# Second encoder layer of the phase attention: one shared PSUM tile for keys and queries, and a Tanh that writes both halves of the partitions

## The chip, the cores and the metric

The kernel runs on one core of a Trainium2 chip. The metric is the device time of one execution in microseconds (us). Before the change it is 3364.57 us, the median of 5 runs (3363.05 to 3370.61).

A core has five engines with instruction queues of their own, each worked off in order: TensorE (PE, matrix products; its weight loads are shown apart as PEld), VectorE (DVE), ScalarE (ACT, which evaluates functions such as Tanh and Gelu), GpSimd (POOL) and SyncE (SP, which here issues most transfers). Products land in PSUM, a memory of 128 partitions that ACT and DVE can read; everything else works in SBUF, also of 128 partitions.

## What is computed

The program is a tokenizer, one transformer layer with window attention and a mixture of experts, and a second layer that consists of a "phase" attention and an LSTM over 569 time steps, for 16 sequences of width 256. The change lies in the phase attention. Cut to what matters:

```python
def encode(W1, b1, W2, b2):                       # W1 256x256, W2 256x64
    h = gelu(x @ W1 + b1)
    return tanh(h @ W2 + b2)
key_phase   = encode(Wk1, bk1, Wk2, bk2) * freq * pi      # freq: 1, 2, 4, 8 by 16 columns
query_phase = encode(Wq1, bq1, Wq2, bq2) * freq * pi
key_phasor  = cos(key_phase)   + 1j * sin(key_phase)
query_conj  = cos(query_phase) - 1j * sin(query_phase)
memory    = cumsum(key_phasor[..., None] * V[:, :, None, :], axis=1)
retrieved = real(sum(memory * query_conj[..., None], axis=2))
...                                               # scaled, normalized, times Wo, added to x
```

Its result, added to the rows and normalized again, is the input of the LSTM:

```python
gates = x_t @ W_ih.T + h @ W_hh.T + b             # for each of 569 steps
i, f, g, o = split(gates, 4)
c = sigmoid(f) * c + sigmoid(i) * tanh(g)
h = sigmoid(o) * tanh(c)
```

## The kernel before

The rows are kept in tiles of 128 rows by 256 columns. For the second layer, the 569 positions are cut into blocks: block 0 of 32 steps, blocks 1 to 8 of 64 steps, block 9 of 25. Chunk 8 of the row tiles holds the short blocks 0 and 9, chunks 0 to 7 hold blocks 1 to 8. A batch is one chunk of 8 of the 16 sequences, so every block is fed by two batches, and a batch is worked by two slots of two row tiles each.

Four kinds of work run together in the last half of the program (from about 1590 us on):

- **front()** (from line 1339), 36 calls: loads two row tiles, adds the experts' outputs, normalizes, turns the tile (`ftr`, `fxT`), and runs the encoders: first layer `ek`/`eq` with Gelu into `gk`/`gq`, then `v`, then the second layer into the PSUM tile `z` (lines 1405 to 1413), Tanh into `y` (named `fy`, line 1416), and three DVE operations that scale, round and subtract (lines 1420 to 1425) and leave the phase in turns in PHI. fronts() then applies Sin to a whole batch of PHI on ACT (line 1635), after a one-element Silu (line 1632).
- **back()** (from line 1472): takes PHI and V of a batch, computes the retrieval as masked products within the tile (`sc`, `w`, `r`) and with the running state S (`ds`), normalizes, multiplies with Wo (`po`), normalizes again and multiplies with W_ih (`xm`); the result `xp` goes to memory as the LSTM's input (`XCD`, `XOD`).
- **steps()**: the LSTM. A step is a chain over PE, ACT and DVE: products of the hidden state with W_hh into the PSUM tiles `gates` and `out_gate` (lines 1741 and 1750) on top of the input that ACT has copied there (lines 1690 and 1695), Tanh of the gates (line 1762) and of the output gate (1770), three DVE operations (1777 to 1790), Tanh of the cell (1798), and the new hidden state `X` (1805). After the Tanh the gates are cleared for the next step by a product with zeros (1684). The input of a block is loaded into `xc` and `xo` once both batches' backs are done with it.
- **sums_of()**: the cumulative sums behind the LSTM.

The order in which these are interleaved is not left to the hardware: class Order is a planner that runs while the program is built. Every piece yields the engine it needs and its cost in us just before its instruction is issued; the planner keeps a time at which each engine becomes free, and always takes the piece that can start first. The LSTM's step has due times of its own (table STEP), and another piece is put ahead of it only if it fits before them, give or take an allowance (`spare`) that depends on how far the backs are ahead of the LSTM. A change of the function table on ACT counts as 1.3 us in the plan. What the plan fixes is the order of instructions on each engine; on the chip each waits for its data by semaphores.

Why the keys' and queries' phases take 128 partitions: cos and sin of the same phase are both needed, and they come from one Sin over 128 partitions, the upper half with a quarter turn added (`off` is 0.25 on partitions 0 to 63 and 0 on 64 to 127). So the 64 values of the second layer have to stand twice, on partitions 0 to 63 and again on 64 to 127. Before the change the product makes both: the weights `Wk2` and `Wq2` are loaded twice side by side into tiles of [128, 2, 2, 64], and product() splits the 128 output partitions into four matmuls of 32 weight columns each (line 1085). z is [128, 2, 256]: 128 partitions, keys and queries side by side, 256 rows of data:

```python
for i, name in enumerate(("k", "q")):
    yield "ACT", 0.45
    nc.scalar.activation(y[:, i, :], z[:, i, :], AF.Tanh, bias=col(f"b{name}2"))
```

The biases' columns (`bk2`, `bq2`) hold the 64 values twice as well.

Of the kernel before, what the change touches and what calls it, by code (L numbers as in the profile page):

```python
# [10 lines left out]
F32 = mybir.dt.float32  # L11
BF16 = mybir.dt.bfloat16
AF = mybir.ActivationFunctionType
# [100 lines left out]
COLUMN = 0.00169  # L114
# [180 lines left out]
def kernel(ctx: ExitStack, tc: tile.TileContext, a: dict, out: bass.AP):  # L295
    nc = tc.nc
# [13 lines left out]
    def col(name, i=0, lo=0, hi=128):  # L310
        return cols[lo:hi, COL[name] + i : COL[name] + i + 1]
# [4 lines left out]
    def frow(name, n=D, at=0):  # L316
        return flow[:, FLOW[name] + at : FLOW[name] + at + n]
# [32 lines left out]
    slot = route.tile([128, NP, 2, NC], F32, name="slot")  # L350
# [635 lines left out]
    l1w = bg.enter_context(tc.tile_pool(name="l1w", bufs=1))  # L986
    Wih = l1w.tile([128, 2, 4 * D], F32, name="W_ih")
    l1 = {n: l1w.tile([128, 2, D], F32, name=n) for n in ("Wk1", "Wq1", "Wv", "Wo")}
    for n in ("Wk2", "Wq2"):
        l1[n] = l1w.tile([128, 2, 2, 64], F32, name=n)  # L990
    masks = l1w.tile([128, 2, 128], F32, name="masks")
    none = l1w.tile([128, 1], F32, name="none")
    S = [l1w.tile([128, 2, 2, D], F32, name=f"S{p}") for p in range(0, NP, 2)]
# [1 line left out]
    def cell_columns(w):  # L995
        return w.rearrange("p (i r) -> p i r", i=2)[:, :, :384].rearrange("p i (a x) -> p i a x", a=4)

    def out_columns(w):
        return w.rearrange("p (i r) -> p i r", i=2)[:, :, 384:]

    def prepare(mo):

        yield "at", ("tile", 0, 1)

        def kxn(n):
            return a[n].rearrange("(k p) n -> p k n", p=128)

        lb = S[0].rearrange("p i k d -> p (i k d)")
        nc.sync.dma_start(lin, kxn("W_lin"))
        for t, of in ((lstm_b, 0), (lb, 1)):  # L1010
            nc.sync.dma_start(t, a["lstm_b"][of].to_broadcast([128, 4 * D]))
        nc.sync.dma_start(Whh, kxn("W_hh"))
        nc.sync.dma_start(Wih, kxn("W_ih"))
        for n in ("Wk1", "Wq1", "Wv", "Wo"):
            nc.sync.dma_start(l1[n], kxn(n))
        for n in ("Wk2", "Wq2"):
            for i in range(2):
                nc.sync.dma_start(l1[n][:, :, i, :], kxn(n))
        nc.sync.dma_start(masks, a["masks"].rearrange("p (i n) -> p i n", i=2))
        yield "at", ("tile", 0, 12)  # L1020
        yield "DVE", 0.2
        nc.vector.tensor_tensor(shut, frow("b_lin", 1), frow("b_lin", 1, 1), ALU.subtract)
        yield "DVE", 0.2
        nc.vector.tensor_scalar(shut, shut, 2.0, None, ALU.mult)
        yield "DVE", 0.2
        nc.vector.tensor_tensor(lin[:, :, :1], lin[:, :, 1:], lin[:, :, :1], ALU.subtract)
        yield "DVE", 0.4
        nc.vector.tensor_copy(wl, lin[:, :, :1].to_broadcast([128, 2, 128]))
        by_unit = [cols[:, COL[n] : COL[n] + 2] for n in ("fw", "bw")]
        yield "DVE", 0.2  # L1030
        nc.vector.tensor_tensor(weights[:, 0, :], by_unit[0], by_unit[1], ALU.subtract)
        for i, of, by in ((0, weights[:, 0, :], 0.5), (1, by_unit[1], -0.5), (2, by_unit[1], 0.5)):
            yield "DVE", 0.2
            nc.vector.tensor_scalar(weights[:, i, :], of, by, None, ALU.mult)
        for t in begins.values():
            yield "POOL", 0.6
            nc.gpsimd.memset(t, 1.0)
            nc.gpsimd.memset(t.rearrange("p (b t) -> p b t", b=NB)[:, :, :1], 0.0)
        for t in XS_OF:
            yield "POOL", 1.0  # L1040
            nc.gpsimd.memset(t.rearrange("p k t x -> p (k t x)"), 0.0)
        yield "POOL", 0.2
        nc.gpsimd.memset(nil, 0.0)
        for t in XO:
            yield "POOL", 0.5
            nc.gpsimd.memset(t.rearrange("p t x -> p (t x)"), 0.0)
        yield "DVE", 0.2
        nc.vector.memset(one3, 1.0)
        nc.vector.memset(none, 0.0)
        yield "DVE", 1.2  # L1050
        nc.vector.tensor_tensor(lstm_b, lstm_b, lb, ALU.add)
        yield "DVE", 0.5
        v = cell_columns(lstm_b)[:, :, :, 64:]
        nc.vector.tensor_scalar(v, v, 2.0, None, ALU.mult)
        for n, t in bias3.items():
            yield "DVE", 0.3
            nc.vector.memset(t, 0.0)
            x = frow(n)[:1]
            pieces = mo.tile([1, 3, D], BF16, name=n + "_pieces", tag="pieces", bufs=1)
            left = S[1][:1, 0, 0, :]  # L1060
            yield "DVE", 1.4
            nc.vector.tensor_copy(pieces[:, 0, :], x)
            nc.vector.tensor_tensor(left, x, pieces[:, 0, :], ALU.subtract)
            nc.vector.tensor_copy(pieces[:, 1, :], left)
            nc.vector.tensor_tensor(pieces[:, 2, :], left, pieces[:, 1, :], ALU.subtract)
            for i in range(3):
                for j in range(2):
                    nc.sync.dma_start(t[i : i + 1, j, :], pieces[:, i, :])

        for k in range(2):
            for v in (cell_columns(Whh[:, k, :])[:, :, :, :64], out_columns(Whh[:, k, :])):
                yield "POOL+", 1.3
                nc.gpsimd.tensor_scalar(v, v, 0.5, None, ALU.mult)
            yield "POOL+", 0.85
            v = cell_columns(Wih[:, k, :])[:, :, :, 64:]
            nc.gpsimd.tensor_scalar(v, v, 2.0, None, ALU.mult)

    def product(out, lhsT, rhs, start, stop):  # L1080


        for m in range(0, out.shape[0], 32):
            own = slice(m, min(m + 32, out.shape[0]))
            nc.tensor.matmul(out[own], lhsT[:, own], rhs, start=start, stop=stop)  # L1085

    def bank(name, slot):
        return ps.tile([128, 512], F32, name=name, tag=f"bank{slot}", bufs=1)
# [178 lines left out]
    def copy(to, src, scale=None, bias=None):  # L1267

        if plan.chosen == "DVE":
            if scale is None:  # L1270
                nc.vector.tensor_copy(to, src)  # L1271
            else:
                nc.vector.tensor_scalar(to, src, scale, bias, ALU.mult, ALU.add)
        elif scale is None:
            nc.scalar.copy(to, src)
        else:
            nc.scalar.activation(to, src, AF.Identity, scale=scale, bias=bias)
# [61 lines left out]
    def front(p, c, n, at, slot):  # L1339

        u = f"{p}_{c}"
# [8 lines left out]
        for j in range(2):  # L1350
            y = wk.tile([128, 2, D], F32, name=f"yg{u}_{j}", tag=f"yg{slot}_{j}")
# [20 lines left out]
        g = {}  # L1372
# [23 lines left out]
        for j in range(2):  # L1396
            for k in range(2):
# [3 lines left out]
                    start=False, stop=(j + k == 2),  # L1401
                )
        yield "DVE/ACT", 0.69, 0.58
        copy(V[:, both, :], v)
        z = bank(f"z{u}", slot).rearrange("p (k n) -> p k n", k=2)
        y = wk.tile([128, 2, 256], F32, name=f"fy{u}", tag=f"xn{slot}")
        for i, name in enumerate(("k", "q")):
            for k in range(2):
                yield "PE", 256 * COLUMN
                product(  # L1410
                    z[:, i, :], l1[f"W{name}2"][:, k].rearrange("p i x -> p (i x)"),
                    g[name][:, k, :], start=(k == 0), stop=(k == 1),
                )
        for i, name in enumerate(("k", "q")):
            yield "ACT", 0.45
            nc.scalar.activation(y[:, i, :], z[:, i, :], AF.Tanh, bias=col(f"b{name}2"))


        yield "DVE+", 0.54
# [200 lines left out]
    def fronts(slot):  # L1620
        for n, (c, p0, late) in enumerate(BATCHES):
            if late:
                continue
            yield "rank", n - 2
            yield from front(p0 + 2 * slot, c, n, 2 * slot, slot)
            batch = batches[n]
            plan.mark(("front", n, slot))
            if slot:
                yield "at", ("front", n, 0)

                yield "ACT", 0.2, "silu"
                nc.scalar.activation(none, none, AF.Silu)
                for i in range(2):
                    yield "ACT", 0.6, "silu"
                    nc.scalar.activation(batch[0][:, i, :], batch[0][:, i, :], AF.Sin, scale=-2.0 * PI_BELOW)
                if c == 8:
                    nc.sync.dma_start(PHD[:, :, 128 * p0 : 128 * p0 + 512], batch[0])
                    nc.sync.dma_start(VD[:, p0 : p0 + 4, :], batch[1])
                plan.mark(("phi", n))
# [283 lines left out]
    n, total = sums[len(RUNS) - 1]  # L1923
# [152 lines left out]
```

## Time and profile before

| what | value |
|---|---|
| median of 5 runs | 3364.57 us |
| the profiled execution, its time | 3363.43 us |
| its span, first to last instruction | 3361.7 us |
| mean granted TensorE clock | 0.978 |
| PE busy | 3058.7 us, 91% of the span |
| PEld busy | 2231.1 us, 66% |
| DVE busy | 2027.6 us, 60% |
| ACT busy | 1470.0 us, 44% |
| POOL busy | 786.3 us, 23% |
| first z product starts at, last | 1601.7 us, 2937.4 us |
| LSTM: first and last Tanh of the gates start at | 1709.7 us, 3317.0 us |

A group's row in the profile names the line, the engine, the operation, what it writes and reads, the shapes and the count; behind the bar stand its busy time, the mean ns of one, and the idle time of its engine just before it with what ended that. Each matmul of this program leaves two records in the trace, so counts of matmuls there are twice those of the program. PE is pipelined: what a row of products takes is best read from where the next one starts, since the ends are modelled and overlap.

### The profile page before, as it was taken

How to read it: one execution, taken by the hardware profiler on the slowest of the kernel's cores; microseconds unless marked ns; L12 is line 12 of the kernel's file. 1: busy time of each engine (PE TensorE's matmuls, PEld its weight loads, DVE VectorE, ACT ScalarE, POOL GpSimd, SP SyncE). 2: the span in 40 equal slices, each digit the busy share in tenths (PEclk: the TensorE clock that was granted, in tenths of full speed). 3: DMA queues.
4: the chain of work that ended last, by engine and by line, in shares of the span. 5: the costliest groups of instructions: out<-in, count | busy, mean ns of one | idle time of the engine just before them, and what ended most of it. 6: DMA issues, size and time to landing. Idle time of an engine off the chain costs nothing.

```text
span 3361.7 us, 134328 instructions
## 1 busy us (share of the span) xinstructions
PE 3058.7 (91%) x57536; PEld 2231.1 (66%) x57536; DVE 2027.6 (60%) x6787; ACT 1470.0 (44%) x5030; POOL 786.3 (23%) x1524
## 2 busy tenths in 40 slices
PE   6999999999759999997899999999999999999884
PEld 3666666666548888886566666766666666666652
DVE  4677777766732222222566777777777777766555
ACT  3545545554412222221443555555555555454442
POOL 1253554444533322222311011000101010100000
PEclk9999999999979999998999999999999999999997
DMA  5111221111176666663333333333323333333333
GB/s 179 53 53 52 88 79 62 48 36 41 42 261 225 226 225 233 225 234 126 112 92 89 93 76 89 83 95 75 98 75 92 83 92 78 76 92 79 90 102 113
DMA packets 276071, 366.81 MB, mean 109 GB/s; under 512 B 144481, under 2 KB 220177, under 8 KB 263313
## 3 DMA queue, kind: packets, MB, share of 16 engines
q1 hardware_dynamic: 249360, 300.91, 30.6%
q0 software_dynamic: 14496, 39.75, 3.1%
q10 hardware_dynamic: 11616, 17.56, 1.8%
q8 instruction: 451, 7.39, 0.9%
q14 instruction: 148, 1.20, 0.1%
HBM read 239.33 MB, written 118.75 MB: 107 GB/s over the span
## 4 chain that ended last, share of the span: by engine, by line
PE 38%; DVE 7%; ACT 4%; issue 2%; DMA 1%; SPq 1%; POOL 0%; ACTq 0%; DVEq 0%
PE gates L1741 13%; PE xm_False L1085 5%; PE out_gate L1750 2%; PE ek L1085 2%; PE z L1085 2%; PE eq L1085 2%; PE po_False L1085 2%; PE ds_False L1085 1%; PE v L1085 1%; ACT act L1762 1%; PE r_False L1085 1%; ACT th L1798 1%; DVE ab L1777 1%; DVE cT L1790 1%; DVE act L1783 1%
## 5 line engine op out<-in xcount | busy, mean ns | idle before, releaser
L1741 PE MATMUL gates<-W_hh,X 128*32 128x96 f32 (+1 forms) x18176 | 488.3, 248 | 63.6 <-DVE X L1805 61.4
L1741 PEld LDWEIGHTS gates<-W_hh,X 128*32 128x32 f32 (+1 forms) x18176 | 374.1, 103 | 257.8 <-DVE X L1805 243.3
L1248 ACT ACTIVATE hT<-hp,w 128x256 f32<-128x256 f32 x316 | 132.3, 471 | 480.4 <-PE hp L1241 313.3
L1762 ACT ACTIVATE act<-gates 128x96 f32<-128x96 f32 x568 | 141.7, 249 | 446.0 <-PE gates L1741 439.0
L1255 PE MATMUL y<-w,hT 128*128 128x256 f32 x1264 | 289.7, 382 | 5.2 <-ACT hT L1248 1.5
L1085 PE MATMUL xm_False<-W_ih,dxT_False 128*32 128x256 f32 x4352 | 292.1, 380 | 2.5 <-DVE dxT_False L1271 1.9
L1241 PE MATMUL hp<-xt,w 128*128 128x256 f32 x1264 | 287.8, 381 | 1.0 <-ACT hT L1248 1.0
L1777 DVE SCALAR_TENSOR_TENSOR ab<-act 128x64 f32<-128x64 f32 x568 | 127.9, 225 | 259.7 <-ACT act L1762 250.1
L1255 PEld LDWEIGHTS y<-w,hT 128*128 128x128 f32 x1264 | 236.8, 190 | 45.2 <-ACT hT L1248 14.4
L1684 PEld LDWEIGHTS <-nil 128*32 128x32 bf16 x4552 | 189.2, 94 | 112.5 <-issue 53.7
L1241 PEld LDWEIGHTS hp<-xt,w 128*128 128x128 f32 x1264 | 240.1, 191 | 35.7 <-ACT hT L1248 1.4
L1184 POOL DMA_INDIRECT YT<-ys,to x158 | 153.3, 970 | 439.6 <-DVE ys L1261 408.1
L1261 DVE TENSOR_TENSOR ys<-y,w 128x512 f32<-128x512 f32 x79 | 54.6, 691 | 316.4 <-PE y L1255 223.9
L1750 PE MATMUL out_gate<-W_hh,X 128*32 128x64 f32 x9088 | 233.7, 220 | 1.7 <-issue 1.7
L1690 ACT COPY gates<-xc 128x96 f32<-128x96 f32 x569 | 138.7, 244 | 185.5 <-DMA xc<-XCD 77.8
L1750 PEld LDWEIGHTS out_gate<-W_hh,X 128*32 128x32 f32 x9088 | 187.4, 110 | 4.8 <-issue 2.0
L1805 DVE SCALAR_TENSOR_TENSOR X<-toT,th 128x32 f32<-128x32 f32 x569 | 109.9, 193 | 120.9 <-ACT th L1798 117.4
L1798 ACT ACTIVATE th<-cT 128x32 f32<-128x32 f32 x569 | 130.5, 229 | 92.5 <-DVE cT L1790 43.3
L1301 POOL TENSOR_SCALAR d_False_rstd<-d_False_mv 128x2 f32<-128x2 f32 (+1 forms) x36 | 9.0, 251 | 675.8 <-DVE d_False_mv L1293 551.5
L908 POOL DMA_INDIRECT XS<-XN,at x144 | 149.0, 1035 | 45.6 <-issue 24.4
L693 PE MATMUL wqk<-wxT,wqkv 128*128 128x128 f32 x1152 | 150.6, 278 | 8.8 <-ACT wxT L687 8.6
L693 PEld LDWEIGHTS wqk<-wxT,wqkv 128*128 128x128 f32 x1152 | 139.4, 192 | 24.9 <-ACT wxT L687 13.5
(356 smaller groups left out, 6498.6 us busy)
## 6 DMA issues: line engine op xcount, KB each, us to landing
w<-in_wpack SPq DMA_DIRECT2D x79, 1154.0 KB
taps<-in_taps SPq DMA_DIRECT2D x16, 1764.0 KB
xc<-XCD SPq DMA_DIRECT2D x71, 384.0 KB
XCD<-xp_False SPq DMA_DIRECT2D x256, 96.0 KB
xs<-XS SPq DMA_DIRECT2D x79, 258.0 KB
yg<-YT SPq DMA_DIRECT2D x72, 256.0 KB
HD<-h SPq DMA_DIRECT2D x72, 128.0 KB
fh<-HD SPq DMA_DIRECT2D x72, 128.0 KB
```

The costliest lines, as they stand in the source:

```text
L693: nc.tensor.matmul(qk[:, j, m, :], wqkv[:, k, D * j + 128 * m : D * j + 128 * m + 128], xT[:, k, :], start=(k == 0), stop=(k == 1),)
L908: fill(0, nc.gpsimd.indirect_dma_start(out=XS[0], out_offset=bass.IndirectOffsetOnAxis(ap=at[:, i, c - lo : c - lo + 1], axis=0), in_=XN[p ...
L1085: nc.tensor.matmul(out[own], lhsT[:, own], rhs, start=start, stop=stop)
L1184: keep(nc.gpsimd.indirect_dma_start(out=YT, out_offset=bass.IndirectOffsetOnAxis(ap=to[:, i : i + 1], axis=0), in_=ys[:, i, :], in_offset= ...
L1241: nc.tensor.matmul(hp[:, i, :], w1[:, k, hc * 128 : (hc + 1) * 128], xT[:, k, :], start=(k == 0), stop=(k == 1),)
L1255: nc.tensor.matmul(y[:, i, :], hT[:, hc, 128 * i : 128 * i + 128], w2[:, hc, :], start=(hc == 0), stop=(hc == 3),)
L1684: nc.tensor.matmul(g[32 * q : 32 * q + 32, :n], nil[:, :32], nil[:, :n], start=True, stop=last)
L1741: nc.tensor.matmul(GC[32 * q : 32 * q + NB * (1 + half), :96], before[:, kk, NB * (1 - half) :], Whh[:, kk, own : own + 96], start=False, ...
L1750: nc.tensor.matmul(GO[32 * q : 32 * q + 32, :64], before[:, kk, :], Whh[:, kk, own : own + 64], start=False, stop=(kk == 1),)
L1762: nc.scalar.activation(act[:, :96], GC[:, :96], AF.Tanh, scale=0.5), begun.pop((k, t))
L1777: nc.vector.scalar_tensor_tensor(ab, act[:, :64].rearrange("p (g x) -> p g x", g=2), 1.0, act[:, 64:].rearrange("p (g x) -> p g x", g=2), ...
L1798: nc.scalar.activation(th.rearrange("p k x -> p (k x)"), cT, AF.Tanh, scale=0.5)
```

## The change

The second layer's weights of keys and queries share one tile, `W2`, keys in columns 0 to 63 and queries in columns 64 to 127; each is loaded once. The product for keys writes partitions 0 to 63 of z and that for queries partitions 64 to 127, so z is [128, 256]. The loop over the two halves of the 256 contracted values (k) is now the outer one. Tanh then reads the 64 partitions of one encoder and is run twice for each: once to the same half of the partitions of y, once to the other half. The planner is told of two pieces of PE work instead of four, and of four on ACT instead of two. What follows (the scaling, rounding and Sin) is the same.

```diff
-    for n in ("Wk2", "Wq2"):
-        l1[n] = l1w.tile([128, 2, 2, 64], F32, name=n)
+    l1["W2"] = l1w.tile([128, 2, 2, 64], F32, name="W2")
...
-        for n in ("Wk2", "Wq2"):
-            for i in range(2):
-                nc.sync.dma_start(l1[n][:, :, i, :], kxn(n))
+        for i, n in enumerate(("Wk2", "Wq2")):
+            nc.sync.dma_start(l1["W2"][:, :, i, :], kxn(n))
...
-        z = bank(f"z{u}", slot).rearrange("p (k n) -> p k n", k=2)
+        z = bank(f"z{u}", slot)[:, :256]
         y = wk.tile([128, 2, 256], F32, name=f"fy{u}", tag=f"xn{slot}")
+        for k in range(2):
+            yield "PE", 256 * COLUMN
+            for i, name in enumerate(("k", "q")):
+                product(
+                    z[64 * i : 64 * i + 64], l1["W2"][:, k, i, :], g[name][:, k, :],
+                    start=(k == 0), stop=(k == 1),
+                )
         for i, name in enumerate(("k", "q")):
-            for k in range(2):
-                yield "PE", 256 * COLUMN
-                product(
-                    z[:, i, :], l1[f"W{name}2"][:, k].rearrange("p i x -> p (i x)"),
-                    g[name][:, k, :], start=(k == 0), stop=(k == 1),
-                )
-        for i, name in enumerate(("k", "q")):
-            yield "ACT", 0.45
-            nc.scalar.activation(y[:, i, :], z[:, i, :], AF.Tanh, bias=col(f"b{name}2"))
+            own = slice(64 * i, 64 * i + 64)
+            for half in (i, 1 - i):
+                yield "ACT", 0.45
+                nc.scalar.activation(
+                    y[64 * half : 64 * half + 64, i, :], z[own], AF.Tanh,
+                    bias=col(f"b{name}2", 0, own.start, own.stop),
+                )
```

Since the planner's input changes, the order of all instructions on PE, DVE and ACT in the last half of the program is planned anew.

## The prediction

> **What bounds the kernel now.** I read the page first, then the kernel in stretches, then the order of time around one stall. From the page's costliest groups and the groups by line, the parts the change touches and the wait that matters:
>
> ```profile
> L1690 ACT COPY gates<-xc 128x96 f32<-128x96 f32 x569 | 138.7, 244 | 185.5 <-DMA xc<-XCD 77.8 <-PE gates L1684 68.2 <-PE out_gate L1684 24.6
> L1085 PE MATMUL z<-gq,Wq 128*32 128x256 f32 x576 | 43.1, 383 | 0.0
> L1085 PE MATMUL z<-gk,Wk 128*32 128x256 f32 x576 | 41.1, 382 | 2.7 <-DVE V L1271 1.5 <-ACT V L1275 1.1
> L1416 ACT ACTIVATE fy<-z,cols 128x256 f32<-128x256 f32 x72 | 30.6, 465 | 11.8 <-PE z L1085 11.7
> ```
>
> Each row: busy us, mean ns of one, idle before it and its cause. z has 1152 records for 36 calls of front(), 32 a call (each written matmul leaves two records); its two Tanh a call take 465 ns each. The first row is the recurrent layer (LSTM) fetching its input: 77.8 us of ACT's idle time there ends with the landing of xc, which the flow (fronts and backs) has to produce. Next, three stretches: inside a block of 64 steps, a block's start, and the end, when no front or back is left.
>
> ```profile
> 2297.00:2357.00 60.00, 56.71 (x1795) 40.49 (x1796) 48.53 (x188) 33.05 (x138) 5.42 (x12) 1.00 0.31 79
> 2369.00:2385.00 16.00, 15.79 (x306) 9.61 (x298) 12.27 (x30) 3.47 (x12) 1.56 (x5) 1.00 0.44 109
> 3200.00:3300.00 100.00, 80.35 (x2616) 54.54 (x2607) 48.60 (x220) 43.32 (x202) 0.00 (x0) 1.00 0.26 74
> ```
>
> Columns: length, busy us of PE, PEld, DVE, ACT, POOL, then the granted clock (1.00 throughout). The cell's Tanh (L1762) starts 40 times in the last stretch, 2.50 us a step, with nothing else to do; inside the block 23 times in 60 us, 2.55 a step, although PE carries all the flow's products. So a step is its own dependency chain, and the flow's products ride in its gaps. But in the second stretch, 16 us, the recurrence stands and PE is 99% busy. In order of time, ACT and then PE:
>
> ```profile
> 2368.93 0.25 ACT L1762 ACTIVATE act<-gates 128x96 f32<-128x96 f32 x1 [1.27 <-PE gates L1741]
> ...
> 2382.63 0.24 ACT L1690 COPY gates<-xc 128x96 f32<-128x96 f32 x1 [11.04 <-DMA xc<-XCD]
> ...
> 2384.84 0.25 ACT L1762 ACTIVATE act<-gates 128x96 f32<-128x96 f32 x1 [0.65 <-PE gates L1741]
> ```
>
> ```profile
> 2371.86 1.91 PE L1085 MATMUL xm_False<-W_ih,dxT_False 128*32 128x256 f32 x32
> 2373.59 1.91 PE L1085 MATMUL ek<-fxT,Wk 128*32 128x256 f32 x32
> ...
> 2383.04 1.07 PE L1085 MATMUL z<-gk,Wk 128*32 128x256 f32 x16 [0.21 <-DVE V L1271]
> 2383.93 0.84 PE L1741 MATMUL gates<-W_hh,X 128*16 128x96 f32 x32
> 2384.81 0.61 PE L1085 MATMUL z<-gq,Wq 128*32 128x256 f32 x8
> ```
>
> The last xm, which the next block's input is made of, ends at 2373.77; the input lands 8.9 us later (9.5 at 2204.63, 10.2 at 1849.46), and PE works off other products meanwhile, z just ahead of the gates. From the starts of L1762, all 568 intervals: 550 last at most 3.2 us (mean 2.57, sum 1412), 18 are longer (sum 196). Seven of these stand before a block: 57.6 us before block 1, then 13.2, 19.2, 15.9, 16.0, 15.9, 15.9; none before block 8. The recurrence starts at 1709.7. So time can be won in two places: that start, and these stalls.
>
> **The change part by part.** *z on PE.* 32 records of 256 columns start 1.73 us apart from the next group (2371.86 to 2373.59). After the change a front issues half of them: 0.87 us less, times 36 = **31.2 us of PE**. No row shows this z, where two strips stream gk and two gq. The bounds: concurrent as now (0.87 a front saved), or the two halves one after the other (nothing saved). I take the first; the gates row L1741 also streams other columns of W_hh into each strip.
>
> *Tanh on ACT.* 72 of 128x256 become 144 of 64x256. Shape prices: 366 ns (L737, a 64x256 copy) to 465 ns (L1416). No row writes another half of the partitions than it reads; below I bound that by nothing and by twice 465. I take 465. Two in a row take 0.84 us, so 36 x 0.84 = **30 us more on ACT**. Cover: in a step ACT is done with the recurrence 1.43 us after L1762's start and next needed at 2.50, free for 1.07 us. 26 ordinary steps carry two Tanh today: median 2.505 us, against 2.504 for the 294 without any flow work on ACT. If that cover went, it would be 0.42 us for each Tanh past it. Behind a Tanh wait the recurrence's next copy and Tanh on ACT, and, through the gates, PE.
>
> The page TensorEngine Tiling (PSUM Bottleneck) of the Trainium skill speaks against the change: a faster TensorE does not speed up reading PSUM out, which may become the limit. By that rule a front's stage goes from 1.73 (PE) to 1.68 (ACT), 2 us in all and not 31.
>
> *Loads.* Two DMAs fewer of 4 among the weights on SP, issued in the expert stage, some 600 us ahead; nothing, since z first runs at 1601.7. If late they would hold the first z.
>
> *The order.* The planner redoes the whole order, as the built instructions show, and this decides. I priced each row of PE's order as above (128-wide turns 0.11 each) and cut it at the gates of each step. Sum from the first front: 825.7 us before, 794.6 after, 31 less as it must be. Where it goes:
>
> - Ordinary steps: 599.6 to 584.7 us. Worth nothing: steps with 0 and with 1.2 to 1.3 us of products both average under 2.58.
> - The start: up to the last xm of block 0, 82.5 to 75.8, so -6.7. But ACT's order there has 16 table loads where there were 8, since Gelu of the next front now stands between the two Sin of a batch. At 1.28 us that is 10.3 us on ACT in two clumps. Ahead of the first's readers PE has some 12 us of other products, and behind the second the input takes 15.3 us to land (last xm 1693.9, copy 1709.2), so both are mostly covered. Bounds -6.7 to +3.6; I take **-5**.
> - The stalls. Products in them (us) against length: 50.6 gives 57.6; 11.3, 13.2; 16.7, 19.2; 13.2, 15.9. So content plus 7 at the first, plus 1.9 to 2.7 elsewhere. New content: 48.3, 9.9, 16.0, 18.4, 16.9, 4.1, 5.8. By these offsets (2.5 for the last two): 55.3, 11.7, 18.5, 21.1, 19.6, 6.6, 8.3; changes -2.3, -1.4, -0.6, +5.2, +3.6, -9.3, -7.6. Before block 8 there is a new one: its last xm now stands one step ahead, not ten. With 9.3 us to land, less the rest of a step, that interval is about 10.3 instead of 2.5: +7.8. Three steps that took 3.8 with a table load and 2.6 us of products lose those products: -2. Sum **-6.6**; -14 if the new one is hidden, -1.5 if the stalls before 6 and 7 stay at 10.
>
> The page ScalarE: Activation LUTs (What ACT_TABLE_LOAD costs) puts a switch at 1283 ns plus a drain of 1380. The trace shows the first and not the second: after the load at 1644.06 the next ACTIVATE starts at 1645.35. By the page the 8 loads would be 21 us, by the row 10.
>
> *Sum:* -5 - 6.6 = -11.6, about -12. The profiled execution took 3363.43 us (span 3361.7 and 1.7 around it), 1.1 under the median: 3351.4 on its scale, **3353** on the median of 3364.57.
>
> **The rivals.**
> *All of it comes back (0.12).* The flow is what the stalls wait for, so 31.2 us less of PE end in them: 3333. For: PE is 99% busy there. Against: the order leaves 15 us of the saving in ordinary steps.
> *No change (0.23).* The table loads eat the gain at the start (0) and the stalls before blocks 6 and 7 wait for transfers at 10 us (-1.5): 3363. The same follows if the mixed strips of z don't run together. For: ACT has 10.3 us more in some 100 us. Against: the cover counted above.
> *Slower (0.10).* A Tanh that reads one half and writes the other takes twice as long, 0.93 us. The order puts two or three Tanh into each of 54 intervals; a pair would take 1.8 and miss the 1.07 free by some 0.75, 40 us in all: 3353 + 40 = 3393. For: no such write in the trace. Against: the plain ones cost no more than a copy. It decides from a pair of about 1.42 us on: 54 x 0.35 = 19 turns -12 into +7.
>
> **How the numbers follow.** Forecast, 0.55: 3353, own range 3344 to 3362. This kernel's measurement can tell about 0.2%, 6.7 us, so faster means under 3357.8, slower over 3371.3. Faster: nine tenths of the forecast, the first rival, and some of the second: 0.65. Same: 0.24. Slower: 0.11. The range reaches down most of the way to the first rival and up past no change: 3336 to 3367; it leaves out the slower rival and the last of the first.
>
> **What would show it.** z with 576 records and some 40 us busy, fy x144 at 0.37 to 0.47 us; L1762's first start at 1700 to 1707; steps still at 2.50 where two Tanh sit; stalls of 19 to 21 us before blocks 4 and 5, under 9 before 6 and 7, about 10 before 8. I am wrong if fy is over 0.6 us, if the start is later than 1710, if the stalls before 6 and 7 stay over 12, or if the mean ordinary step moves from 2.57 by over 0.02 (11 us).

## The result, and the profile after

The changed kernel takes 3375.92 us, the median of 28 runs (3368.41 to 3382.92); the kernel before, run beside it, 3367.83 us (50 runs, 3362.89 to 3373.82). The ratio is 1.0022, 95% interval 1.0016 to 1.0027: slower by some 8 us, where 12 us faster were forecast. The profiled execution took 3380.62 us, with a span of 3378.8 us.

The page of the changed kernel first: the engines, and the recurrence's fetch of its input.

```profile
PE 3048.7 (90%) x56960; PEld 2223.8 (66%) x56960; DVE 2020.9 (60%) x6780; ACT 1524.9 (45%) x5117; POOL 791.5 (23%) x1524
...
L1693 ACT COPY gates<-xc 128x96 f32<-128x96 f32 x569 | 138.7, 244 | 159.4 <-PE gates L1687 68.3
```

PE is busy for 10 us less than before, ACT for 55 more. Its wait for the input (77.8 us before) is no longer the first cause in the copy's row; in the view of waits it comes to 54.2.

The two parts that the change touches, from the groups by line and from the answer on the tile `fy` (durations min/median/max, then first and last start):

```profile
L1083 PE MATMUL z<-gk,W 128*32 128x256 f32 x288 | 40.7, 381 | 1.2 <-DVE V L1269 1.2
L1083 PE MATMUL z<-gq,W 128*32 128x256 f32 x288 | 40.7, 381 | 0.0
```

```profile
L1416 ACT ACTIVATE fy<-z,cols x144: 453/469/473, 1611.8 to 2957.8; 64x256 f32<-64x256 f32 x144
```

And one half of a front's z in order of time on PE, in the changed kernel:

```profile
1797.47 0.39 PE L1083 MATMUL z<-gk,W 128*32 128x256 f32 x2
1797.48 0.39 PE L1083 MATMUL z<-gq,W 128*32 128x256 f32 x2
1797.68 0.39 PE L1083 MATMUL z<-gk,W 128*32 128x256 f32 x2
1797.70 0.39 PE L1083 MATMUL z<-gq,W 128*32 128x256 f32 x2
1797.90 0.61 PE L1083 MATMUL eq<-fxT,Wq 128*32 128x256 f32 x8
```

Keys and queries start 0.01 us apart, so strips with different data run together, and 8 records last 0.43 us to the next product: 0.87 a front instead of 1.73. The saving on PE is there in full, and a Tanh that crosses the halves costs 469 ns, not 930. Neither of the hardware questions of the prediction is the cause.

Where the time went, from the starts of the gates' Tanh (L1762 before, L1765 after) in the two profiled executions. "Start" runs from the first turn of a front (ftr) to the first of these Tanh:

```
us                                            before     after   difference
before the first ftr                         1589.59   1598.14    +8.6
start                                         120.16    116.27    -3.9
the eight intervals before blocks 1 to 8       156.1     153.9    -2.2
the other 560 intervals                       1451.2    1467.3   +16.1
behind the last Tanh                           44.62     43.22    -1.4
```

The first line is of this one execution (its granted clock up to 953 us is 0.96 against 0.98): ahead of it the change leaves out two weight loads and nothing else, and over the profiles of all kernels here, on several chips, the first ftr starts anywhere between 1589.6 and 1606.2 us. The rest sums to +8.6, close to the +8.1 of the medians. So the loss sits in the ordinary steps, which the prediction had priced at nothing. Split by what ACT does in them, as the sum of what each lasts over 2.505 us (the last row: single intervals of 4 to 9 us that stand before no block):

```
ordinary steps, us over 2.505 each     before   after
with a Tanh of a front                    2.5     7.5
with a table load                        15.1    12.3
all others                               25.2    32.0
single long intervals                     5.5    12.7
```

The long ones first. The view of waits from 1700 to 3340 us, before and then after (us in all, times, longest):

```profile
DVE xp_False L1591 <- DMA XOD<-xp_False: 3.0, 1, 3.0
```

```profile
DVE xp_False L1594 <- DMA XOD<-xp_False: 13.7, 4, 5.1
...
PEld sc_False L1083 <- DVE xp_False L1594: 5.6, 4, 4.6
```

The changed kernel's longest ordinary interval, 8.72 us, in order of time:

```profile
2828.07 0.25 ACT L1765 ACTIVATE act<-gates 128x96 f32<-128x96 f32 x1 [1.30 <-PE gates L1744]
...
2832.57 0.61 SPq L1599 DMA_DIRECT2D XCD<-xp_False  x1
2832.58 0.69 DVE L1594 TENSOR_TENSOR xp_False<-xm_False,lstm_b 128x512 f32<-128x512 f32 x1 [5.06 <-DMA XOD<-xp_False]
2833.19 0.22 DVE L1780 SCALAR_TENSOR_TENSOR ab<-act 128x64 f32<-128x64 f32 x1
...
2833.97 0.23 ACT L1801 ACTIVATE th<-cT 128x32 f32<-128x32 f32 x1 [4.85 <-DVE cT L1793]
```

DVE stands for 5.06 us at xp, until a store of an earlier xp has left its buffer: xp has two buffers for each slot, and SP, which issues one store per 0.6 us, is behind. DVE works in order, so the recurrence's own operation (L1780), whose input was there at 2828.3, waits behind it. The planner's account has no term for SP and none for xp's buffers, so it doesn't see this.

By the starts of the steps, only two of these four waits lie in ordinary intervals, 2.8 us in the one of 6.80 and 5.1 us in this one of 8.72. The other two, 5.9 us, lie in the stall before block 1, as does the one of before.

Now steps with Tanh, ACT alone, first before the change:

```profile
1945.07 0.25 ACT L1762 ACTIVATE act<-gates 128x96 f32<-128x96 f32 x1 [1.09 <-PE gates L1741]
...
1946.42 0.83 ACT L1416 ACTIVATE fy<-z,cols 128x256 f32<-128x256 f32 x2
1947.58 0.25 ACT L1762 ACTIVATE act<-gates 128x96 f32<-128x96 f32 x1 [0.33 <-PE gates L1741]
```

And a pair of steps in the changed kernel:

```profile
1954.73 0.94 ACT L1416 ACTIVATE fy<-z,cols 64x256 f32<-64x256 f32 x2
1955.88 0.25 ACT L1765 ACTIVATE act<-gates 128x96 f32<-128x96 f32 x1 [0.21 <-PE gates L1744]
1956.11 0.22 ACT L1773 ACTIVATE to<-out_gate 128x64 f32<-128x64 f32 x1
1956.36 0.47 ACT L1416 ACTIVATE fy<-z,cols 64x256 f32<-64x256 f32 x1
1956.85 0.24 ACT L1693 COPY gates<-xc 128x96 f32<-128x96 f32 x1
1957.12 0.23 ACT L1801 ACTIVATE th<-cT 128x32 f32<-128x32 f32 x1
...
1957.48 0.47 ACT L1416 ACTIVATE fy<-z,cols 64x256 f32<-64x256 f32 x1
1957.98 0.56 ACT L1275 ACTIVATE rxn_False<-r_False,rxn_False_less,r_False_rstd 128x256 f32<-128x256 f32 x1
1958.55 0.25 ACT L1765 ACTIVATE act<-gates 128x96 f32<-128x96 f32 x1
```

The first two Tanh lie in the free end of a step and cost nothing. The third stands ahead of the recurrence's copy, which starts 0.97 us after L1765's Tanh, and the fourth behind it; this step lasts 2.67. Over the whole run, 20 steps have their Tanh at these two places (0.5 and 1.6 us after L1765); their median is 2.66, that of the 16 with two Tanh at 1.4 and 1.8 is 2.50. Also, two Tanh take 0.94 us and not 0.83 as before: they no longer overlap.

### The profile page after: what moved, and what is told of

It reads as the page before. It is cut to its first block, busy times and chain, and to the rows that moved or that the text cites. A ratio compares the mean times of both kernels' runs of the same rounds, so it can differ in the third digit from the quotient of the medians.

```text
span 3378.8 us, 133265 instructions
## 1 busy us (share of the span) xinstructions
PE 3048.7 (90%) x56960; PEld 2223.8 (66%) x56960; DVE 2020.9 (60%) x6780; ACT 1524.9 (45%) x5117; POOL 791.5 (23%) x1524
## 4 chain that ended last, share of the span: by engine, by line
PE 34%; DVE 8%; ACT 6%; issue 2%; DMA 1%; SPq 1%; POOL 1%; ACTq 0%; DVEq 0%; POOLq 0%
PE gates L1744 12%; PE xm_False L1083 6%; PE out_gate L1753 2%; PE po_False L1083 2%; PE v L1083 2%; ACT th L1801 2%; ACT act L1765 2%; PE ek L1083 2%; DVE ab L1780 1%; DVE cT L1793 1%; PE ds_False L1083 1%; DVE X L1808 1%; DVE act L1786 1%; PE eq L1083 1%; PE r_False L1083 1%
## 5 line engine op out<-in xcount | busy, mean ns | idle before, releaser
L1744 PE MATMUL gates<-W_hh,X 128*16 128x96 f32 (+1 forms) x18176 | 489.6, 248 | 75.4 <-DVE X L1808 69.8
L1744 PEld LDWEIGHTS gates<-W_hh,X 128*16 128x16 f32 (+1 forms) x18176 | 375.0, 103 | 265.0 <-DVE X L1808 246.4
L1765 ACT ACTIVATE act<-gates 128x96 f32<-128x96 f32 x568 | 142.2, 250 | 425.5 <-PE gates L1744 418.2
L1780 DVE SCALAR_TENSOR_TENSOR ab<-act 128x64 f32<-128x64 f32 x568 | 127.8, 225 | 266.2 <-ACT act L1765 259.5
L1687 PE MATMUL gates<-nil 128*32 128x96 bf16 x2276 | 131.0, 210 | 23.6 <-ACT act_init L1765 3.6
```

The costliest lines, as they stand in the source:

```text
L1687: nc.tensor.matmul(g[32 * q : 32 * q + 32, :n], nil[:, :32], nil[:, :n], start=True, stop=last)
L1744: nc.tensor.matmul(GC[32 * q : 32 * q + NB * (1 + half), :96], before[:, kk, NB * (1 - half) :], Whh[:, kk, own : own + 96], start=False, ...
L1765: nc.scalar.activation(act[:, :96], GC[:, :96], AF.Tanh, scale=0.5), begun.pop((k, t))
L1780: nc.vector.scalar_tensor_tensor(ab, act[:, :64].rearrange("p (g x) -> p g x", g=2), 1.0, act[:, 64:].rearrange("p (g x) -> p g x", g=2), ...
```

## The experiments

Every time is compared with the kernel before on the same chip, whose median ranged from 3365.8 to 3382.9 us; "against before" is the difference of the two medians. Totals are taken from the timed runs and only steps from the profiles: the profiled execution of e3 was 12 us above its median, that of e1 5.

**e1 to e4: the buffer of xp, and the Tanh.** The third buffer of xp leaves the order of the instructions on PE, DVE, ACT and POOL as it is. e1 is the changed kernel with it, e4 the kernel before with it:

```diff
-            xp = wk.tile([128, 512], F32, name=f"xp{u}_{i}", tag=f"xp{slot}", bufs=2)
+            xp = wk.tile([128, 512], F32, name=f"xp{u}_{i}", tag=f"xp{slot}", bufs=3)
```

> The changed kernel with a third buffer for xp, the tile that DVE writes for each 512 columns of the LSTM's input and SP stores; the order on PE, ACT and DVE stays as it was, only the wait for a free buffer goes. Theory (two causes: DVE waits for xp buffers, and the third Tanh sits ahead of the recurrence's copy): the two long ordinary intervals of 6.8 and 8.7 us fall under 3.2, DVE's wait for XOD before L1594 falls from 13.7 us to under 3, and the time falls by 8 to 11 us, to between -3 and 0 against before. Rival (the four Tanhs alone cost the time): the time stays at +8. Rival (a new order costs some us everywhere, no single place): the long intervals stay or move elsewhere, +4 to +8.

> The kernel before with a third buffer for xp. Theory: in its order DVE waits only 3.4 us for a buffer in all, so 0 to -3 us. Rival (the third buffer helps any order by what it helps the changed kernel): -8 or more.

e2 keeps the changed kernel's order and its z, but runs two Tanh of 128 partitions at the places of the first and the third, so half of its phases are those of the other encoder; e3 has the third buffer too:

```diff
                 yield "ACT", 0.45
-                nc.scalar.activation(
-                    y[64 * half : 64 * half + 64, i, :], z[own], AF.Tanh,
-                    bias=col(f"b{name}2", 0, own.start, own.stop),
-                )
+                if half == i:
+                    nc.scalar.activation(y[:, i, :], z, AF.Tanh, bias=col(f"b{name}2"))
```

> The changed kernel in its own order, but with two Tanhs of 128x256 in the places of the first and third, and none in those of the second and fourth; each reads the whole of z, so half of the phases are those of the other encoder. Theory: the 29 intervals with a Tanh between the output gate's Tanh and the input copy return from 2.66 to about 2.50 us or keep one such Tanh of 365 to 465 ns: 3 to 6 us less in all, +2 to +5 against before; the two long intervals stay at 6.8 and 8.7. Rival (waits for xp buffers are the whole cost): +8 as the changed kernel. Rival (Tanhs are the whole cost): 0 against before or less.

> Both edits together (third buffer for xp; two Tanhs of 128x256, values of half the phases wrong). Theory: the two causes add up, 13 to 17 us less than the changed kernel: -5 to -9 against before, which is the gain at the start, at the stalls and at the end alone. Rival (the causes hide one another, or neither is one): within 4 us of the better of the two single edits.

Measured: e1 3361.41, against before -4.3, ratio 0.9988 (0.9979 to 0.9997). e4 3363.04, -2.7, 0.9990 (0.9981 to 0.9999). e2 3364.74, -1.0, 0.9997 (0.9987 to 1.0006). e3 3355.96, -9.8, 0.9971 (0.9961 to 0.9982). In e1 DVE no longer waits for a store at xp_False between 1700 and 3340 us; what is left there is the wait for the product:

```profile
DVE xp_False L1594 <- PE xm_False L1083: 18.1, 21, 2.3
```

The buffer takes 12 us from the changed kernel (+8.1 to -4.3, each against the kernel before beside it) and 8.8 from e2 (on one chip), but only 2.7 from the kernel before: the new order ran into a limit that the old one hardly touched. The two extra Tanh are worth 9.1 us (e2) or 5.5 (e3 against e1, one chip). e4 came as expected, e1 and e3 gained about 1 us more than their ranges, and e2 missed: +2 to +5 was expected, and -1.0 is what its second rival gave, that the Tanh are the whole cost. That rival doesn't hold alone, since e1 keeps the four Tanh and gains more. But the two gains are not apart: singly they come to 12.4 and 9.1, together to 17.9, so some 3.6 us are counted in both. In e2 the Tanh at the third's place costs nothing, in ACT's order of time:

```profile
1946.83 0.25 ACT L1763 ACTIVATE act<-gates 128x96 f32<-128x96 f32 x1 [0.69 <-PE gates L1742]
1947.05 0.22 ACT L1771 ACTIVATE to<-out_gate 128x64 f32<-128x64 f32 x1
1947.17 0.47 ACT L1417 ACTIVATE fy<-z,cols 128x256 f32<-128x256 f32 x1
1947.53 0.25 ACT L1691 COPY gates<-xc 128x96 f32<-128x96 f32 x1
```

It starts 0.12 us behind its neighbour and the copy 0.36 behind it; in the changed kernel these are 0.25 and 0.49 for a Tanh of the same 0.47. The copy comes 0.70 us after the gates' Tanh instead of 0.97, and the 26 such steps have a median of 2.50.

**e5 to e8: the order by itself.** e5 does the old work (four products of z and two Tanh of 128 partitions) in the changed kernel's order; e6 the new work in the order before. In e7 and e8 the work is that of before, and only one cost told to the planner is another:

```diff
         for i, name in enumerate(("k", "q")):
+            yield "PE", 256 * COLUMN
             for k in range(2):
-                yield "PE", 256 * COLUMN
                 product(
...
         for i, name in enumerate(("k", "q")):
-            yield "ACT", 0.45
-            nc.scalar.activation(y[:, i, :], z[:, i, :], AF.Tanh, bias=col(f"b{name}2"))
+            for half in (i, 1 - i):
+                yield "ACT", 0.45
+                if half == i:
+                    nc.scalar.activation(y[:, i, :], z[:, i, :], AF.Tanh, bias=col(f"b{name}2"))
```

> The kernel before (four products of z a front over 128 partitions, two Tanhs of 128x256) with all other instructions on PE, ACT and DVE in exactly the order of the changed kernel. Theory (the new order costs 10 us through xp waits, the Tanhs 5, and 31 us less of PE are worth little): the two intervals of 6.8 and 8.7 us are there, the third Tanh's delay is not, and PE has 31 us more: +8 to +20 against before. Rival (the new order is not to blame, the new instructions are): within 3 us of before.

```diff
-            yield "PE", 256 * COLUMN
+            for i, name in enumerate(("k", "q")):
+                yield "PE", 256 * COLUMN
...
+            yield "ACT", 0.45
             for half in (i, 1 - i):
-                yield "ACT", 0.45
                 nc.scalar.activation(
```

> The changed kernel's products and four Tanhs with all other instructions in exactly the order of the kernel before; the four Tanhs of a front stand where two pairs stood. Theory: no long xp waits; the gain of PE shows only where PE sets the pace (-2 to -6 us at the start); four Tanhs of 0.475 us do not fit in the 1.07 us that ACT has free in a step, so each front adds 0.3 to 0.8 us: 0 to +20 in all, by Tanhs alone. Rival (order alone matters, Tanhs are hidden): 0 to -6 against before.

```diff
-            yield "ACT", 0.45
+            yield "ACT", 0.50
```

> The kernel before, unchanged in its work, with the planner told 0.50 us instead of 0.45 for each Tanh of the encoders: another order of the same instructions. Theory (where xp waits and table loads fall is an accident of the order): between -8 and +10 us, not zero, and the difference is found in a few long intervals. Rival (the plan is stable, and only the changed instructions moved the time): within 2 us of before.

```diff
-                yield "PE", 256 * COLUMN
+                yield "PE", 240 * COLUMN
```

> The kernel before, unchanged in its work, with the planner told 240 columns instead of 256 for each product of z: a third order of the same instructions. Theory: as for the one before, between -8 and +10 us. Rival: within 2 us of before.

Measured, against a median before of 3377.48: e5 3395.03, +17.6, ratio 1.0059 (1.0045 to 1.0072). e6 3398.35, +20.9, 1.0069 (1.0055 to 1.0083). e7 3393.40, +15.9, 1.0052 (1.0038 to 1.0066). e8 3455.62, +78.1, 1.0233 (1.0219 to 1.0247). e5 fell into its range and e6 just above. e7 and e8 were far outside what was expected of them: one planned cost raised by 11% or lowered by 6% makes the same work slower. In e7 the intervals before blocks 1 to 8 sum to 163.2 us (156.1 before) and the other 560 to 1459.4 (1451.2): the loss is in both. In e8 DVE's wait for stores grows to 48.7 us, from 3.0:

```profile
DVE xp_False L1591 <- DMA XOD<-xp_False: 48.7, 20, 5.7
```

Besides, its intervals before blocks 3 to 7 are 22 to 27 us. In e5 a front's Tanh waits for z, by the answer on the tile `fy`, then in ACT's order of time:

```profile
  PE z L1085: 29.7, 34
```

```profile
1952.97 0.47 ACT L1418 ACTIVATE fy<-z,cols 128x256 f32<-128x256 f32 x1 [0.39 <-PE z L1085]
1954.06 0.25 ACT L1764 ACTIVATE act<-gates 128x96 f32<-128x96 f32 x1 [0.62 <-PE gates L1743]
```

The order was planned for 0.87 us of z and meets 1.73; such steps last 3.12, and steps with a Tanh sum to 16.3 us over 2.505 each. So e5 is not the price of an order alone: it is a price of work that doesn't fit the plan. With it, z's saving can be read at a fixed order, the one planned for the halved z: e5 against e2, 18.6 us (two chips). And in e6 the four Tanh come where two were planned, in a row of 1.91 us. The step shown takes 3.59, with one more copy of the flow in it; the 28 ordinary steps with a front's four Tanh have a median of 3.34:

```profile
1947.56 0.25 ACT L1766 ACTIVATE act<-gates 128x96 f32<-128x96 f32 x1 [1.03 <-PE gates L1745]
...
1949.21 1.91 ACT L1417 ACTIVATE fy<-z,cols 64x256 f32<-64x256 f32 x4
1951.15 0.25 ACT L1766 ACTIVATE act<-gates 128x96 f32<-128x96 f32 x1
```

**e9 to e11: the third Tanh moved, and the buffer again.** e10 issues the third Tanh at the place of the fourth, everything else in the changed kernel's order; e9 has the third buffer too, and e11 is e5 with the third buffer.

```diff
                 yield "ACT", 0.45
-                nc.scalar.activation(
-                    y[64 * half : 64 * half + 64, i, :], z[own], AF.Tanh,
-                    bias=col(f"b{name}2", 0, own.start, own.stop),
-                )
+                for to in ((half,) if i == 0 else () if half == 1 else (1, 0)):
+                    nc.scalar.activation(
+                        y[64 * to : 64 * to + 64, i, :], z[own], AF.Tanh,
+                        bias=col(f"b{name}2", 0, own.start, own.stop),
+                    )
```

> The same move of the third Tanh with xp buffers as they were. Theory: 3 to 6 us less than the changed kernel, +2 to +5 against before, the waits for xp still there. Rival (the gain with two Tanhs of 128 partitions came from fewer Tanhs, not from their place): +8 as the changed kernel.

> The changed kernel, all of its work, with the third xp buffer and with the third Tanh of a front moved on ACT to just before the fourth, so that none stands between the output gate's Tanh and the copy of the next input; all other instructions in the changed kernel's order. Theory: the 29 intervals of about 2.66 us go to 2.50 to 2.55, the long xp waits are gone: 15 to 19 us less than the changed kernel, -7 to -11 us against the kernel before. Rival (the Tanh's delay only moves to the next step): as with the third buffer alone, -4.

> The work of the kernel before in the order of the changed one, with the third xp buffer. Without it this order cost 17.6 us. Theory (xp waits are the larger part of what the order costs): 9 to 13 us less, +5 to +9 against before. Rival (the order costs because it was planned for less PE work): within 3 us of +17.

Measured, against 3375.81: e10 3380.31, +4.5, ratio 1.0016 (1.0007 to 1.0025). e9 3374.95, -0.9, 0.9995 (0.9986 to 1.0004). e11 3386.05, +10.2, 1.0031 (1.0019 to 1.0043). e10 lies within the range expected of it, but its interval doesn't part it from the changed kernel's (1.0016 to 1.0027), and in its trace the steps with a Tanh sum to 8.8 us over 2.505 each, against 7.5 in the changed kernel: the move is not shown to gain anything. e9 missed: it gained 5.4 over e10 by the buffer, but was not better than e1. Its steps with nothing but two Tanh are at 2.51 now, but the 22 that hold another operation of ACT besides the pair average 2.85 (2.75 in e1): the delay had only moved. So it is not the third Tanh's place alone that costs, but that ACT has four Tanh without overlap to fit in. e11 ended 1.2 us above its range; against e3 it gives z's saving a second time, 20.0 us.

**e12 and e13: why the narrow Tanh don't overlap.** One execution each, with four Tanh in a row at the fourth's place, so that the values of some phases are wrong. In e12, slot 0 runs the changed kernel's four, slot 1 two of 128 partitions and two on partitions 0 to 63:

```diff
...
+                if slot == 0:
+                    for n, m, to in ((0, "k", 0), (0, "k", 1), (1, "q", 0), (1, "q", 1)):
+                        own = slice(64 * n, 64 * n + 64)
+                        nc.scalar.activation(
+                            y[64 * to : 64 * to + 64, n, :], z[own], AF.Tanh,
+                            bias=col(f"b{m}2", 0, own.start, own.stop),
+                        )
+                else:
+                    for n, m in ((0, "k"), (1, "q")):
+                        nc.scalar.activation(y[:, n, :], z, AF.Tanh, bias=col(f"b{m}2"))
+                    for n, m in ((0, "k"), (1, "q")):
+                        nc.scalar.activation(
+                            y[:64, n, :], z[:64], AF.Tanh, bias=col(f"b{m}2", 0, 0, 64)
+                        )
```

> One look at how Tanhs follow each other on ACT: in one slot the four of 64 partitions of the changed kernel, in the other two of 128 partitions, then two of 64 that read the same half and write the same half (values of that slot are wrong). In the changed kernel those of 64 start 0.48 us apart, in the kernel before those of 128 start 0.37 us apart. Theory (64 partitions are what loses the overlap): 128 after 128 at 0.37, 64 after 64 of the same half at 0.48. Rival (the change of the half on the input or output side loses it): 64 after 64 of the same half at 0.37.

Its time was 3399.59. ACT in order of time, a front of slot 0 (with what follows it) and one of slot 1:

```profile
1715.39 1.91 ACT L1421 ACTIVATE fy<-z,cols 64x256 f32<-64x256 f32 x4
1717.33 0.25 ACT L1777 ACTIVATE act<-gates 128x96 f32<-128x96 f32 x1
...
1739.95 0.82 ACT L1427 ACTIVATE fy<-z,cols 128x256 f32<-128x256 f32 x2
1740.67 0.82 ACT L1429 ACTIVATE fy<-z,cols 64x256 f32<-64x256 f32 x2
1741.39 0.24 ACT L1777 ACTIVATE act<-gates 128x96 f32<-128x96 f32 x1
```

The four of slot 0 take 1.91 us, 0.48 apart, and none of the 54 neighbouring pairs overlaps; the four of slot 1 start 0.36 apart throughout, the ones of 64 partitions too (18 of 18). So it is not the number of partitions. e13 puts the narrow pair on partitions 64 to 127, read from the same half in slot 0 and from the other half in slot 1:

```diff
...
+                for n, m in ((0, "k"), (1, "q")):
+                    nc.scalar.activation(y[:, n, :], z, AF.Tanh, bias=col(f"b{m}2"))
+                own = slice(64, 128) if slot == 0 else slice(0, 64)
+                for n, m in ((0, "k"), (1, "q")):
+                    nc.scalar.activation(
+                        y[64:, n, :], z[own], AF.Tanh, bias=col(f"b{m}2", 0, own.start, own.stop)
+                    )
```

> The four Tanh of a front stand in a row at the place of the changed kernel's fourth. In both slots the first two are of 128 partitions, and then come two of 64 partitions that write partitions 64 to 127; in slot 0 they read 64 to 127 too, in slot 1 they read 0 to 63. So the phases of partitions 64 to 127 are those of one encoder for keys and queries, and those of 0 to 63 of the keys' product for both: the output is not the reference's there. Seen so far: a 64x256 Tanh that reads or writes from partition 64 starts 0.475 us after its neighbour, one that reads and writes from 0 starts 0.365 after it. Theory: an ACT instruction waits for the end of the one before whenever its input or its output starts on another partition than that one's did. Then the step from the second to the third Tanh is 0.475 in both slots, and from the third to the fourth 0.365 in both, since nothing changes between them. Rival: instructions that touch partitions from 64 on never overlap. Then the step from the third to the fourth is 0.475 too, in slot 0 and in slot 1. A second rival, that it is the crossing of the halves, gives 0.365 within slot 0 and 0.475 within slot 1. The time says little: about 20 us over the kernel before, as for the other kernel with four Tanh in a row.

Its time was 3409.50 (3382.91 for the kernel before on that chip). A front of slot 0, then one of slot 1:

```profile
1959.48 0.82 ACT L1419 ACTIVATE fy<-z,cols 128x256 f32<-128x256 f32 x2
1960.34 0.83 ACT L1422 ACTIVATE fy<-z,cols 64x256 f32<-64x256 f32 x2
1961.19 0.47 ACT L1383 ACTIVATE gq<-eq,cols 128x256 f32<-128x256 f32 x1
...
1970.29 0.83 ACT L1419 ACTIVATE fy<-z,cols 128x256 f32<-128x256 f32 x2
1971.14 0.83 ACT L1422 ACTIVATE fy<-z,cols 64x256 f32<-64x256 f32 x2
```

In both slots the narrow pair takes 0.83 us for two, so it overlaps (0.37 apart, 36 of 36), and what stands 0.49 apart is the step from the wide pair to the narrow one (36 of 36) and from there to the next instruction. Both rivals fall: these ACT instructions wait for the end of the one before where their input or their output starts on another partition than that one's. The output alone changes at the step from the wide pair in slot 1 of e13, and the input alone from the second to the third of e6's four in a row, which start 12 to 13 ns behind the end of the one before (29 of 29). Starts on partitions 0 and 64 are all that was tried. Each of the changed kernel's four is held behind its neighbour by this, but for the first.

## Why the prediction was wrong, step by step

*The step that failed* is "Ordinary steps: 599.6 to 584.7 us. Worth nothing". They became 16.1 us longer in the profile. Four things are in it. The single long intervals (+7.2) are DVE's waits for stores of xp: shown by the wait lines and by e1, where the two of 6.80 and 8.72 us are gone. The steps with a Tanh (+5.0) are the four narrow Tanh, which lose their overlap on ACT, most of all where the third stands ahead of the copy: shown by the step lines, by e2, where a wide Tanh at that place costs nothing, and, for the mechanism, by e6, e12 and e13. Steps with a table load give back 2.8; the prediction had booked that as -2 among the stalls. And 6.8 us lie in all the other steps. This last part stays in e1 and e3 (29.3 and 31.8 us against 25.2), with the old order it is 26.7 in e4, and it was not settled; the profiled clock from 1700 to 1850 us was 0.97 against 0.99 before, which may be some of it.

The evidence offered for the step did not bear it. That a step doesn't feel 1.3 us of products on PE says nothing of its queues on DVE and ACT, and the order there was new as well. One wait of DVE for a store, 3.0 us, was in the trace before; it was not asked what would set its number. The prediction's own sign for this step would not have warned either: the mean of the steps of up to 3.2 us went from 2.567 to 2.582, less than the 0.02 it named, since the store waits fall on two single intervals outside that mean.

*Tanh on ACT: the duration right, the pair wrong.* 465 was taken and 469 measured, but "two in a row take 0.84" was taken from 128-wide neighbours; the pair takes 0.94. The trace before had the row that fits: 66 pairs of the 64x256 copies of L737, which write one half and then the other, start 12 ns (median) behind the end of the first, where the Tanh of 128 partitions overlap by 100. The planner gave them too little as well: it takes 0.1 us off each ACT instruction for the overlap (`OVERLAP`). "0.42 us for each Tanh past" the cover was also too high: a third one cost 0.16, since most of it still found room.

*z on PE: right*, 0.87 us a front. At a fixed order it was worth 18.6 and 20.0 us of its 31.2.

*The start: right.* -3.9 against -5. L1765's first start came at 1714.4, over the 1710 named as a sign of error, but 8.6 us of that are older than the first front.

*The stalls: right from block 2 on, wrong at the first.* Intervals before blocks 1 to 8:

```
predicted   55.3  11.7  18.5  21.1  19.6   6.6   8.3  10.3
measured    61.4  11.2  19.0  20.2  19.2   6.0   7.4   9.5
```

The content of PE's order between two gates gives a stall to within 1 us, but at the first it missed by 6. There e5, with the old work in this order, shows 62.3, and e6, with the new work in the old order, 58.2 (57.6 before): this comes with the order. The 5.9 us that DVE waits for stores in this stall don't explain it, since without them it still lasts 60.0 in e1 and 61.4 in e3; the cause stays open. Measured sum -2.2; predicted, without the three steps with a table load, -4.6.

*The rivals.* None of them happened as written. The slower one needed a Tanh of twice the length; that the narrow Tanh are dearer was right in direction only. None named the stores, though SP's queue lies on the path that the flow feeds. The Trainium skill's page TensorEngine Tiling (PSUM Bottleneck), weighed in the prediction, was nearer than the forecast in kind, though not in size: of the some 19 us that z's halving is worth here, reading PSUM with more instructions took back 5.5 to 9.

*The sum.* e3, which has almost no store waits at xp and two wide Tanh in place of the four, is at -9.8, inside the forecast's own range; it is no kernel to use, since half of its phases are wrong. With the third buffer throughout, the parts are: the order with the old work +12.9 (e11 against e4), z -20.0, the two extra Tanh +5.5, together -1.6 (e1 against e4; the steps cross two chips). The changed kernel with a third buffer of xp, -4.3, beats both kernels; that it beats the kernel before with the same buffer (-2.7) is not shown, their intervals overlap.

## What to carry to other kernels

Where a planner lays out all queues, a change of costs is a change of order, and the order has to be priced on every queue and every buffer that the planner does not account for, not on the engine that got faster alone. Test the limits that lie outside the plan first: here one more buffer took 12 us from the changed kernel, more than the 8 that the edit had cost it. And a result split over partition halves should be priced with the pair's spacing from a row that also changes its first partition, not from the duration of one instruction.

## What was not expected of the hardware

- ACT: neighbouring Tanh that start on the same partitions overlap by 0.09 to 0.12 us, of 128 or of 64 partitions; where the first partition of input or output changes between 0 and 64, the second starts 12 to 26 ns after the first has ended (e6, e12, e13). The Trainium skill's page ScalarE: Activation LUTs (What ACT_TABLE_LOAD costs) has the overlap, as some 93 ns, without this exception. Its page VectorE: DVE Perf Modes (Two Vector instructions with no wait between them) has a model for VectorE by which an instruction is held until every earlier one has finished if an input begins in another group of 32 partitions than the last input read from the same memory, or its output in another than the last output into that memory. For starts on 0 and 64, ACT does the same here; other starts were not tried.
- The same work in another order of the same queues cost 16 us more (e7) or 78 (e8).
